# The last sequence's GEGLU in two parts, and the steps of the sequence before it drawn into the last slots

## The chip, the cores and the metric

The kernel runs on one NeuronCore of a Trainium2 chip, in one launch. The metric is the device time of a whole execution, in microseconds (us); where several runs are given, it is their median. The engines are TensorE (PE, with its weight loads PEld), VectorE (DVE), ScalarE (ACT), GpSimd (POOL) and SyncE (SP), each of which takes its instructions in the order in which the program issues them.

## What is computed

The input x is 4 sequences of 512 tokens with 128 features, float32. It is cut here to what matters:

```python
x = x + attention(layernorm(x), Wq, Wk, Wv, Wr)     # 16 heads of 64, causal penalty
y = layernorm(x)
for i in range(6):
    y = local_attention_layer(shift_tokens(y), Wqkv[i], ...) + y   # windows of 32 tokens
    y = ffn_layer(shift_tokens(y), ...) + y
return x + y

def ffn_layer(x, g, bln, W1, b1, W2, b2):
    mu = x.mean(-1, keepdims=True)
    var = ((x - mu) ** 2).mean(-1, keepdims=True)
    xn = (x - mu) / jnp.sqrt(var + 1e-05) * g + bln
    a, gate = jnp.split(xn @ W1 + b1, 2, -1)        # 341 columns each
    return a * jax.nn.gelu(gate, approximate=False) @ W2 + b2
```

`shift_tokens` takes the upper 64 features of a token from the token before it in the same sequence. So the FFN of a tile of tokens needs the tile itself and the last column of the tile before it.

## The kernel before

Stage 1 (to about 590 us) is the first attention layer. It isn't touched. Stage 2 is the six layers. Its work is cut into 96 units, one for each layer, sequence and tile of 128 tokens (6 x 4 x 4), numbered in this order; `u.T` is the tile within its sequence. Activations lie transposed, features on the partitions and tokens along the free axis: `xT[b]` is 128 x 512.

The order of the work is written out by hand. `slot(n, ...)` issues, in a software pipeline, the attention of unit n (scores, softmax, times_v), the projections and rotations of unit n+2, the transposes of q and k of unit n+1, and the output projection (`project_out_2`, L633) and residual (L641) of unit n-1. `scores` (L565, L576) ends with two DVE operations, the row maximum mx (L586) and the subtraction to pr (L588); then ACT takes the exponent (L594), PE transposes pr (L538, the helper `transposed`, whose copies on ACT are L541), and `times_v` (L608, and on DVE L617, L618) forms the output, which `transpose_o` transposes into aT.

The rotations of unit n+2 run on DVE (L463, L467) and POOL (L478 adds the two halves, L486 multiplies with the inverse norm; both on 128 x 1024). POOL also takes the 12 operations (L82 to L85) of the inverse root of the norms and the carry of k (L557). `rsqrt` is three Newton steps: two integer operations on DVE, then four operations three times on the engine given.

The FFN of a sequence (class `Ffn`) is seven steps over all four tiles at once, one step in each slot after the sequence's last unit n (in slots n+1 to n+7): `shift` (POOL, L416 to L418), `mean` (PE L93, DVE L95, ACT Square L97), `var` (PE L102, DVE L104 and the 14 operations of `rsqrt`), `scale` (PE L110, DVE L114, L116) together with GEGLU chunk 0, chunk 1, chunk 2, and `out`. A chunk is two matmuls (L666 for the gate, L667), a Gelu on ACT (L669) and a multiply on DVE (L671); chunks have 128, 128 and 85 rows. Each 128 x 512 float32 matmul is two passes in the trace. `out` is three matmuls (L680) and an addition (L682). In the last layer, `finish` follows it: an addition of x1T (L691), four transposes (L694), a copy on ACT (L696) and a store of 256 KB on SP (L697). Gelu and Exp need different tables of ACT, so a change from one to the other brings an ACT_TABLE_LOAD.

In a slot, `shift`, `mean`, `var` and `scale` stand after the residual, that is behind mx and pr of the slot's unit; the chunks and `out` stand at the slot's end, before `transpose_o`. The slots run to 102. Sequence 22 (layer 5, b = 2) shifts in slot 92 and ends in 98; sequence 23 shifts in slot 96, when all attention is issued, and ends in 102. From slot 94 on there is no unit n+2 left to project. In the profile, slot 94 begins at 2246.7 us (L565) and slot 95 at 2265.25.

PSUM: `one_t` gives one of two banks in turn, `two_t(k, ...)` one of three pairs of banks, counted from n. SBUF: `tmpt` gives one of 7 tiles in turn; the tags rot, t1 and pr have 6, 3 and 2 tiles of 128 x 1024.

Of the kernel before, what the change touches and what calls it, by code (L numbers as in the profile page):

```python
# [8 lines left out]
F32 = mybir.dt.float32  # L9
BF16 = mybir.dt.bfloat16  # L10
I32 = mybir.dt.int32
AF = mybir.ActivationFunctionType
ALU = mybir.AluOpType
# [18 lines left out]
def body(ctx: ExitStack, tc: tile.TileContext, a, out: bass.AP):  # L32
# [16 lines left out]
    def tmpt(n=S):  # L49
        return tmp.tile([P, n], F32, tag="tmp", name="tmp_t")  # L50
# [22 lines left out]

    def rsqrt(v, n, eng):

        y = small.tile([P, n], F32, tag=f"y{n}", name="y")
        t = small.tile([P, n], F32, tag=f"yt{n}", name="yt")
        ti = t.bitcast(I32)
        nc.vector.tensor_scalar(ti, v.bitcast(I32), 1, None, ALU.logical_shift_right)  # L79
        nc.vector.tensor_scalar(y.bitcast(I32), ti, -1.0, 1597463007.0, ALU.mult, ALU.add)  # L80
        for k in range(3):
            eng.tensor_tensor(t, y, y, ALU.mult)  # L82
            eng.tensor_tensor(t, t, v, ALU.mult)
            eng.tensor_scalar(t, t, -0.5, 1.5, ALU.mult, ALU.add)
            eng.tensor_tensor(y if k < 2 else v, y, t, ALU.mult)  # L85

    def layernorm_steps(state, bank, inT, outT, g=None, b=None):

        def mean():
            m = bank()
            mm(m, lhsT=avg, rhs=inT(), start=True, stop=True)  # L93
            xc = state["xc"] = tmpt()
            nc.vector.tensor_tensor(xc, inT(), m, ALU.subtract)  # L95
            sq = state["sq"] = tmpt()
            nc.scalar.activation(sq, xc, AF.Square)  # L97

        def var():
            v = bank()  # L100
            for t in range(NT):
                mm(v[:, t : t + 1], lhsT=state["sq"][:, t * P : (t + 1) * P], rhs=avg[:, 0:1], start=True, stop=True)  # L102
            rs = state["rs"] = small.tile([P, NT], F32, tag="rs", name="rs")
            nc.vector.tensor_scalar(rs, v[:, 0:NT], EPS, None, ALU.add)  # L104
            rsqrt(rs, NT, nc.vector)

        def scale():
            bc = bank()
            for t in range(NT):
                nc.tensor.transpose(  # L110
                    bc[:, t * P : (t + 1) * P], state["rs"][:, t : t + 1].to_broadcast([P, P]), ident
                )
            h = state["h"] = outT()
            nc.vector.tensor_tensor(h, state["xc"], bc, ALU.mult)  # L114
            if g is not None:
                nc.vector.tensor_scalar(h, h, g, b, ALU.mult, ALU.add)  # L116

        return mean, var, scale
# [13 lines left out]
    with tc.tile_pool(name="s1", bufs=1) as s1, tc.tile_pool(  # L132
# [71 lines left out]
        class Rows:  # L204


            def __init__(self, b, c, t):
                self.b, self.c, self.t = b, c, t
# [202 lines left out]
    def flat(pt):  # L411
        return pt.rearrange("p a n -> p (a n)")

    def shift_into(dst, src):

        nc.gpsimd.memset(dst[HD:P, 0:1], 0.0)  # L416
        nc.gpsimd.tensor_copy(dst[0:HD, :], src[0:HD, :])
        nc.gpsimd.tensor_copy(dst[HD:P, 1:S], src[HD:P, 0 : S - 1])  # L418

    def layer_tables(i):  # L420

# [222 lines left out]


    class Ffn:
        def __init__(self, i, b):
            self.i, self.b, self.us, self.st = i, b, [], {}
            self.mean, self.var, self.scale = layernorm_steps(
                self.st,  # L650
                one_t,
                lambda: self.xs,
                lambda: s2.tile([P, S], F32, tag="hT", name="hT", bufs=2),
                vecs[:, i, 0:1],
                vecs[:, i, 1:2],
            )

        def shift(self):
            self.xs = tmpt()
            shift_into(self.xs, xT[self.b])  # L660

        def chunk(self, f):
            i, (f0, fn), h = self.i, FCH[f], self.st["h"]
            w1 = ffn_w[0][0]
            gp = two_t(0, "ps_proj")
            mm(gp[0:fn, 0, :], lhsT=w1[:, DH + f0 : DH + f0 + fn], rhs=h, start=True, stop=True)  # L666
            mm(gp[0:fn, 1, :], lhsT=w1[:, f0 : f0 + fn], rhs=h, start=True, stop=True)  # L667
            g = tmpt()
            nc.scalar.activation(g[0:fn, :], gp[0:fn, 0, :], AF.Gelu, bias=vecs[0:fn, i, 6 + f : 7 + f])  # L669
            u = tmpt()  # L670
            nc.vector.scalar_tensor_tensor(  # L671
                u[0:fn, :], gp[0:fn, 1, :], vecs[0:fn, i, 3 + f : 4 + f], g[0:fn, :], ALU.add, ALU.mult
            )
            self.us.append(u)

        def out(self):
            w2 = ffn_w[0][1]
            y = two_t(0, "ps_proj")[:, 0, :]
            for f, (f0, fn) in enumerate(FCH):
                mm(y, lhsT=w2[0:fn, f, :], rhs=self.us[f][0:fn, :], start=(f == 0), stop=(f == len(FCH) - 1))  # L680
            xn = new_xT()
            nc.vector.scalar_tensor_tensor(xn, y, vecs[:, self.i, 2:3], xT[self.b], ALU.add, ALU.add)  # L682
            xT[self.b] = xn
            if self.i + 1 == L:
                self.finish(xn)
            elif self.b + 1 == B:
                ffn_w[0] = load_ffn(self.i + 1)

        def finish(self, xn):
            fin = tmpt()  # L690
            nc.vector.tensor_tensor(fin, x1T[self.b], xn, ALU.add)  # L691
            op = one_t()
            for t in range(NT):
                nc.tensor.transpose(op[:, t * P : (t + 1) * P], fin[:, t * P : (t + 1) * P], ident)  # L694
            ot = tmpt()
            nc.scalar.copy(ot, op)  # L696
            nc.sync.dma_start(  # L697
                out=out[self.b].rearrange("(t p) e -> p t e", p=P),
                in_=ot.rearrange("p (t e) -> p t e", e=EMB),
            )  # L700

# [25 lines left out]
        if u.b + 1 == B and u.T + 1 == NT and u.i + 1 < L:  # L727
            wpart[j] = load_part(u.i + 1, j)

    def slot(n, now, last):  # L730

        u, prev, nxt, new = unit(n), unit(n - 1), unit(n + 1), unit(n + 2)
        T = n % NT
        part[0] = n % 3
        begin(unit(n + 4))
        if u:
# [11 lines left out]
            sum_squares(new, 0)  # L750
        if prev:
            residual(prev)
        if now and T > 0:
            (now.mean, now.var, now.scale)[T - 1]()
        if now and T == 0:
            now.shift()
        if new:
            rotate(new, 0)
            do_project(new, 2)
# [23 lines left out]
            over_norm(new, 1)  # L783
        if nxt:
            carry_k(nxt, follower(nxt))
        if now and T == 3:
            now.chunk(0)
        if last:
            (lambda: last.chunk(1), lambda: last.chunk(2), last.out)[T]()
        if u:  # L790
            transpose_o(u)

    with tc.manual_schedule():
        begin(units[0])
        ffns = {}
        late = norm_x1(one_t, B - 1)
        for n in range(-2, len(units) + NT + 3):
            if -2 <= n < 1:
                late[n + 2]()
            q = n // NT - 1  # L800
            if n % NT == 0 and 0 <= q < L * B:
                ffns[q] = Ffn(units[n - 1].i, units[n - 1].b)
            slot(n, ffns.get(q), ffns.pop(q - 1, None) if n % NT == 2 else ffns.get(q - 1))

def _constants(n):

# [90 lines left out]
```

## Time and profile before

| | |
|---|---|
| time, median of 3 runs | 2316.82 us (2313.41 to 2319.04) |
| time of the profiled execution | 2314.14 us |
| its span, first to last instruction | 2312.4 us |
| mean granted TensorE clock | 0.993 |
| PE, DVE, ACT, POOL busy | 95%, 74%, 56%, 62% of the span |
| output stores | 4 of 256 KB, on SP |

The end of the span, by stretches (us busy of each engine, and the clock granted to TensorE as a share of full speed):

| stretch | PE | DVE | ACT | POOL | clock |
|---|---|---|---|---|---|
| 2240 to 2250 | 9.26 | 7.48 | 7.08 | 5.03 | 1.00 |
| 2250 to 2260 | 8.83 | 8.22 | 4.28 | 5.09 | 1.00 |
| 2260 to 2270 | 8.09 | 4.03 | 1.87 | 0.09 | 0.83 |
| 2270 to 2280 | 7.58 | 2.99 | 3.30 | 0.00 | 0.66 |
| 2280 to 2290 | 9.62 | 3.43 | 3.65 | 1.22 | 1.00 |
| 2290 to 2300 | 6.51 | 4.67 | 0.87 | 0.00 | 0.85 |
| 2300 to 2313 | 6.86 | 3.69 | 2.36 | 0.00 | 0.89 |

A line of the timeline has the start, the duration (of a merged group: to the end of its last), the engine, the line of the code, the operation, what it writes and reads, shapes and count. A line of the chain has start, duration, engine, what is written, line and count. The busy time of PE isn't work at full rate: at half the clock the same matmul counts twice as long.

### The profile page before, as it was taken

What the parts mean: (1) busy time and instruction counts of PE and PEld (TensorE: products, weight loads), DVE (VectorE), ACT (ScalarE), POOL (GpSimd) and SP (SyncE); (2) the same over time, 40 slices, a digit from 0 to 9 for tenths busy, and PEclk for the clock granted to TensorE, in tenths of its full rate; (3) what the DMA queues carried; (4) which work ended last, traced back from release to release, by engine and by line L of the source; (5) the groups of instructions that cost most, each with busy time, mean ns of one, the idle gap of its engine ahead of it and who ended that gap; (6) DMA issues with size and microseconds to landing.
All of it is one profiled execution on the core that took longest, in us unless ns stands there. A gap on an engine that the chain in (4) does not pass through costs nothing.

```text
span 2312.4 us, 81596 instructions
## 1 busy us (share of the span) xinstructions
PE 2201.3 (95%) x35088; PEld 1447.7 (63%) x35088; DVE 1710.5 (74%) x2692; ACT 1301.7 (56%) x2166; POOL 1436.1 (62%) x1897
## 2 busy tenths in 40 slices
PE   6999999999799999999999999999999999999997
PEld 3555555555366666666666666666666666666664
DVE  3665656656678788878877888877888788878773
ACT  2554544445255666666666666666566666566662
POOL 1443444444577777766767766767776767766760
PEclk9999999999999999999999999999999999999998
DMA  3000000000222233222322223223332223322220
GB/s 113 1 1 1 1 1 1 1 1 1 46 69 68 63 90 75 62 69 65 90 71 65 71 66 90 68 63 73 73 89 62 71 62 86 80 62 72 66 56 15
DMA packets 91025, 125.81 MB, mean 54 GB/s; under 512 B 25262, under 2 KB 39468, under 8 KB 90668
## 3 DMA queue, kind: packets, MB, share of 16 engines
q1 hardware_dynamic: 90236, 119.02, 21.0%
q8 instruction: 279, 4.57, 0.9%
q10 hardware_dynamic: 432, 1.57, 0.2%
q14 instruction: 78, 0.64, 0.1%
HBM read 20.41 MB, written 1.05 MB: 9 GB/s over the span
## 4 chain that ended last, share of the span: by engine, by line
PE 81%; DVE 14%; ACT 2%; issue 2%; POOL 1%; DMA 1%; SPq 0%; POOLq 0%; ACTq 0%
PE ps_proj L442 19%; PE ps_one L538 13%; PE ps_one L633 7%; PE ps_att L608 6%; PE ps_att L576 6%; PE ps_sc L216 5%; PE ps_o L287 5%; PE ps_pt L270 3%; PE ps_proj L666 3%; PE ps_proj L667 3%; PE ps_proj L680 2%; DVE yt L79 2%; PE ps_sc L229 2%; DVE t L467 2%; DVE rot L463 2%
## 5 line engine op out<-in xcount | busy, mean ns | idle before, releaser
L478 POOL TENSOR_TENSOR rot<-rot,t 128x1024 f32<-128x1024 f32 x192 | 453.9, 2364 | 193.9 <-DVE t L467 188.6
L442 PE MATMUL ps_proj<-wqkv,xs 128*128 128x512 f32 x1152 | 557.5, 607 | 15.3 <-DVE t L467 5.4
L259 POOL TENSOR_TENSOR pr<-pr,den 128x1024 f32<-128x1024 f32 x128 | 240.9, 1893 | 335.3 <-DVE den L256 333.1
L453 ACT ACTIVATE sq<-ps_proj 128x1024 f32<-128x1024 f32 x192 | 196.9, 1025 | 365.9 <-PE ps_proj L442 329.3
L486 POOL TENSOR_TENSOR rot<-rot,ss 128x1024 f32<-128x1024 f32 x192 | 365.4, 1903 | 15.0
L442 PEld LDWEIGHTS ps_proj<-wqkv,xs 128*128 128x128 f32 x1152 | 200.0, 192 | 179.6 <-issue 156.6
L458 DVE TENSOR_REDUCE ss<-sq 128x16 f32<-128x1024 f32 x192 | 233.1, 1214 | 51.4 <-ACT sq L453 50.7
L241 DVE TENSOR_REDUCE nm<-ps_sc 128x2 f32<-128x1024 f32 x128 | 156.0, 1218 | 118.7 <-PE ps_sc L229 118.7
L463 DVE TENSOR_TENSOR rot<-ps_proj,lt 128x1024 f32<-128x1024 f32 x192 | 233.4, 1216 | 0.0
L467 DVE TENSOR_TENSOR t<-ps_proj,lt 128x1024 f32<-128x1024 f32 x192 | 232.8, 1213 | 0.0
L274 ACT COPY pT<-ps_pt 128x512 f32<-128x512 f32 x128 | 75.2, 588 | 264.6 <-PE ps_pt L270 262.9
L633 PEld LDWEIGHTS ps_one<-aT,wo 128*128 128x128 f32 x1536 | 186.3, 192 | 45.3 <-issue 44.5
L538 PE MATMUL ps_one<-ident,rot 128*128 128x128 f32 x1536 | 210.2, 280 | 2.9 <-issue 1.5
L586 DVE TENSOR_REDUCE mx<-ps_att 128x16 f32<-128x1024 f32 x96 | 117.5, 1224 | 97.1 <-PE ps_att L576 95.3
L633 PE MATMUL ps_one<-aT,wo 128*128 128x128 f32 x1536 | 187.3, 275 | 0.4 <-ACT aT L541 0.4
L247 ACT ACTIVATE pr<-ps_sc,nm 128x512 f32<-128x512 f32 x256 | 175.0, 694 | 16.3 <-DVE nm L241 16.3
L82 POOL TENSOR_TENSOR yt<-y 128x32 f32<-128x32 f32 x288 | 68.9, 239 | 181.8 <-DVE y L80 166.6
L538 PEld LDWEIGHTS ps_one<-ident,rot 128*128 128x128 f32 x1536 | 164.4, 141 | 22.1 <-issue 4.6
L608 PEld LDWEIGHTS ps_att<-vw,pT 64*32 64x32 f32 x9216 | 104.0, 106 | 95.5 <-ACT pT L541 54.0
L270 PEld LDWEIGHTS ps_pt<-ident,pr 128*128 128x128 f32 x1024 | 120.0, 142 | 55.9 <-issue 45.8
L608 PE MATMUL ps_att<-vw,pT 64*32 64x65 f32 x9216 | 129.6, 226 | 26.4 <-DVE t L467 15.9
L520 ACT COPY vt<-ps_proj 128x512 f32<-128x512 f32 x192 | 103.1, 589 | 83.2 <-PE ps_proj L442 82.1
(127 smaller groups left out, 4014.8 us busy)
## 6 DMA issues: line engine op xcount, KB each, us to landing
vw<-vt SPq DMA_DIRECT2D x1152, 65.0 KB
vw_first<-vt SPq DMA_DIRECT2D x336, 65.0 KB
wqkv<-in_wqkv_dram SPq DMA_DIRECT2D x18, 512.0 KB
wo<-in_wo_dram SPq DMA_DIRECT2D x6, 512.0 KB
w<-in_w_dram SPq DMA_DIRECT2D x6, 341.0 KB
xr<-in_x_dram SPq DMA_DIRECT2D x4, 256.0 KB
out_dram<-tmp_t SPq DMA_DIRECT2D x4, 256.0 KB
w<-in_w_dram SPq DMA_DIRECT2D x12, 64.0 KB
```

What stands on the lines that cost most here:

```text
L259: nc.gpsimd.tensor_tensor(self.pr, self.pr, self.den.unsqueeze(2).to_broadcast([P, 2, S]), ALU.mult)
L270: nc.tensor.transpose(pt[:, k * P : (k + 1) * P], self.pr[:, h, k * P : (k + 1) * P], ident)
L442: mm(p[:, c, :], lhsT=u.xs[:, u.T * P : (u.T + 1) * P], rhs=wpart[j][:, c * 512 : (c + 1) * 512], start=True, stop=True,)
L453: nc.scalar.activation(u.sq, u.p[j], AF.Square)
L458: nc.vector.tensor_reduce(u.ss[:, j * HEADS : (j + 1) * HEADS], heads(u.sq), AX.X, ALU.add)
L463: nc.vector.tensor_tensor(heads(t0), heads(pf), lt[:, u.T, 2 * j].unsqueeze(1).to_broadcast([P, HEADS, HD]), ALU.mult)
L467: nc.vector.tensor_tensor(t1.rearrange("p (h t d) -> p h t d", t=2, d=half), pf.rearrange("p (h t d) -> p h t d", t=2, d=half)[:, :, ::-1, :],
L478: nc.gpsimd.tensor_tensor(u.r[j], u.r[j], u.t1, ALU.add)
L486: nc.gpsimd.tensor_tensor(heads(u.r[j]), heads(u.r[j]), u.ss[:, j * HEADS : (j + 1) * HEADS].unsqueeze(2).to_broadcast([P, HEADS, HD]), AL ...
L538: nc.tensor.transpose(tp[:, c * P : (c + 1) * P], src[:, (4 * g + c) * P : (4 * g + c + 1) * P], ident)
L608: mm(o[j * W : (j + 1) * W, h, c * (HD + 1) : (c + 1) * (HD + 1)], lhsT=u.pT[h * HD : (h + 1) * HD, 4 * g + c, j * W : (j + 1) * W], rhs=u ...
L633: mm(y[:, 0:P], lhsT=wo_w[0][:, c, :], rhs=u.aT[:, c, :], start=(c == 0), stop=(c == NC - 1))
```

## The change

`Ffn` takes a range of tiles (`t0`, `nt`), the tiles that it writes to, and the engine of its inverse root; chunks and `out` take the number of their pair of PSUM banks. The steps stand in two tables, `norm` (after the residual) and `geglu` (at the slot's end), filled by `plan`. Up to sequence 21 they stand where they stood.

Sequence 22: `shift` in slot 92 and `mean` in 93 as before; `var` at the end of slot 93 (before: after the residual of 94); `scale` in slot 94, chunks 0 and 1 at the end of 94, chunk 2 at the end of 95, `out` in slot 96.

Sequence 23 is two objects. `most` is its first three tiles: `shift` after the residual of slot 95, `mean` at the end of 95, the rest in slot 96, its inverse root on POOL. `last` is the last tile, all in slot 96, its inverse root on DVE. Their steps are interleaved as the four lines with `plan(norm, end, ...)` say (`end` is 96). Slot 96 is the last. They write to tiles of the tags rot, t1 and pr. `finish` adds in place. The stores become two of 256 KB, one of 192 KB and one of 64 KB. By the listing of each engine's instructions, ACT has two table loads more (Gelu in slot 94, and Exp after it).

```diff
     def rsqrt(v, n, eng):
-        y = small.tile([P, n], F32, tag=f"y{n}", name="y")
-        t = small.tile([P, n], F32, tag=f"yt{n}", name="yt")
+        m = max(n, NT)
+        y = small.tile([P, m], F32, tag=f"y{m}", name="y")[:, 0:n]
+        t = small.tile([P, m], F32, tag=f"yt{m}", name="yt")[:, 0:n]
...
-            rs = state["rs"] = small.tile([P, NT], F32, tag="rs", name="rs")
-            nc.vector.tensor_scalar(rs, v[:, 0:NT], EPS, None, ALU.add)
-            rsqrt(rs, NT, nc.vector)
+            rs = state["rs"] = small.tile([P, NT], F32, tag="rs", name="rs")[:, 0:nt]
+            nc.vector.tensor_scalar(rs, v[:, 0:nt], EPS, None, ALU.add)
+            rsqrt(rs, nt, eng)
...
         def shift(self):
-            self.xs = tmpt()
-            shift_into(self.xs, xT[self.b])
+            n, c0 = self.nt * P, self.t0 * P
+            xs, src = self.temp()[:, 0:n], self.u.xn
+            if c0 == 0:
+                shift_into(xs, src[:, 0:n], n)
+            else:
+                nc.gpsimd.tensor_copy(xs[0:HD, :], src[0:HD, c0 : c0 + n])
+                nc.gpsimd.tensor_copy(xs[HD:P, :], src[HD:P, c0 - 1 : c0 + n - 1])
+            self.xs = xs
...
         def finish(self, xn):
-            fin = tmpt()
-            nc.vector.tensor_tensor(fin, x1T[self.b], xn, ALU.add)
+            n, nt, t0 = self.nt * P, self.nt, self.t0
+            nc.vector.tensor_tensor(xn, x1T[self.b][:, t0 * P : t0 * P + n], xn, ALU.add)
...
-        if now and T > 0:
-            (now.mean, now.var, now.scale)[T - 1]()
-        if now and T == 0:
-            now.shift()
+        for f in norm:
+            f()
...
-        if now and T == 3:
-            now.chunk(0)
-        if last:
-            (lambda: last.chunk(1), lambda: last.chunk(2), last.out)[T]()
+        for f in geglu:
+            f()
         if u:
             transpose_o(u)
...
+        f = Ffn(units[end - NT - 1])
+        plan(norm, end - 4, f.shift)
+        plan(norm, end - 3, f.mean)
+        plan(geglu, end - 3, f.var)
+        plan(norm, end - 2, f.scale)
+        plan(geglu, end - 2, at(f.chunk, 0, 2), at(f.chunk, 1, 0))
+        plan(geglu, end - 1, at(f.chunk, 2, 2))
...
+        def halves(k):
+            t = s2.tile([P, INNER], F32, tag="t1", name="t1", bufs=3)
+            return t[:, 0:S], t[:, S : 2 * S]
...
+        most = Ffn(units[end - 2], 0, NT - 1, big, halves, nc.gpsimd)
+        last = Ffn(units[end - 1], NT - 1, 1, big, sixths)
+        plan(norm, end - 1, most.shift)
+        plan(geglu, end - 1, most.mean)
+        plan(norm, end, last.shift, most.var, at(f.out, 2), most.scale, last.mean, at(most.chunk, 0, 0))
+        plan(norm, end, last.var, at(most.chunk, 1, 1), at(most.chunk, 2, 2), last.scale)
+        plan(norm, end, at(most.out, 0), at(last.chunk, 0, 1), at(last.chunk, 1, 2), at(last.chunk, 2, 0))
+        plan(norm, end, at(last.out, 1))
+        for n in range(-2, end + 1):
             if -2 <= n < 1:
                 late[n + 2]()
-            q = n // NT - 1
-            if n % NT == 0 and 0 <= q < L * B:
-                ffns[q] = Ffn(units[n - 1].i, units[n - 1].b)
-            slot(n, ffns.get(q), ffns.pop(q - 1, None) if n % NT == 2 else ffns.get(q - 1))
+            slot(n, norm.get(n, ()), geglu.get(n, ()))
```

Here `big` gives a tile of the tag rot and `sixths` pairs of 128 columns of one tile of the tag pr; `at(f, *args)` is a call put off.

## The prediction

> **What bounds the kernel now.** I read the page first (PE 95% busy), then the chain of work that ended last, then the timeline of the last 65 us. Up to about 2246 us the two kernels issue the same instructions in the same order, by the listing of each engine's instructions, so only the end can differ. There the chain runs, from 2248.85:
>
> ```profile
> 2248.85 1.24 DVE mx L586
> 2250.11 1.24 DVE pr L588
> 2251.37 1.07 ACT pr L594
> 2252.48 0.67 PE ps_one L538 x4
> ...
> 2258.30 2.63 PE ps_proj L680 x6
> ...
> 2267.37 1.24 DVE mx L586
> ...
> 2278.76 1.48 PE ps_proj L667 x2
> ...
> 2308.56 0.59 ACT tmp_t L696
> ```
>
> Columns: start, duration, engine, what it writes. Without new projections to fill it, PE waits for the softmax of units 94 and 95: from mx to the transposes of pr 3.63 us (2248.85 to 2252.48). The start of mx in slots 94 and 95 therefore sets the end.
>
> The timeline of the same place shows what DVE's small operations meet beside long POOL ones:
>
> ```profile
> 2246.89 0.75 DVE L671 SCALAR_TENSOR_TENSOR tmp_t<-ps_proj,vecs,tmp_t 85x512 f32<-85x512 f32 x1
> 2248.63 1.90 POOL L486 TENSOR_TENSOR rot<-rot,ss 128x1024 f32<-128x1024 f32 x1
> 2250.49 2.35 POOL L478 TENSOR_TENSOR rot<-rot,t 128x1024 f32<-128x1024 f32 x1
> 2251.78 1.08 DVE L79 TENSOR_SCALAR yt<-rs 128x4 int32<-128x4 int32 x1
> 2252.90 0.17 DVE L80 TENSOR_SCALAR y<-yt 128x4 int32<-128x4 int32 x1
> 2252.92 1.91 POOL L486 TENSOR_TENSOR rot<-rot,ss 128x1024 f32<-128x1024 f32 x1
> 2253.11 1.74 DVE L82 TENSOR_TENSOR yt<-y 128x4 f32<-128x4 f32 x1
> 2254.78 0.39 POOL L557 COPY kT<-kT 128x256 f32<-128x256 f32 x1
> 2254.88 0.30 DVE L83 TENSOR_TENSOR yt<-yt,rs 128x4 f32<-128x4 f32 x1
> ```
>
> L79 and L82, 0.17 us elsewhere, last until the POOL operation beside them ends (2252.84, 2254.83). This is the variance step of sequence 22. Its 15 DVE operations take 5.6 us here (2251.58 to 2257.17), and 2.93 us for sequence 23, when POOL is idle (2289.56 to 2292.49). In this place the hold costs nothing: mx has already gone.
>
> Last, single microseconds of PE (PE busy, granted clock, then DMA):
>
> ```profile
> 2262.00:2263.00 1.00, 0.42 (x3) 0.90 0.00 0
> 2263.00:2264.00 1.00, 1.00 (x7) 0.50 0.00 0
> 2277.00:2278.00 1.00, 1.00 (x2) 0.50 0.09 16
> ```
>
> The clock is halved over 2262.9-2266.1, 2273-2279.9 and 2297-2300.3: after each longer idle stretch of PE.
>
> **What the Trainium skill says.** "SBUF — State Buffer", Who interferes with whom: a DVE operation with two SBUF inputs, or in a two-port mode, and a GpSimd operation exclude each other for the whole instruction. The trace agrees: L79 has a median of 1.585 us over 32 instances, against 0.17. "TensorE: Matmul & The Clock Gate", Part 1: the clock is gated to half after an idle window and restored after a busy one, on a free-running grid of 3.41 us. The trace agrees: the changes lie 3.2, 6.9, 6.9, 17.1 and 3.3 us apart, near multiples of 3.41. Where the grid will lie after the change is not known; I keep that of before and give both ends. "ScalarE: Activation LUTs", What ACT_TABLE_LOAD costs: each change of table set is an instruction of ACT; the trace has 1.28 us.
>
> **The change, part by part.** I cut the chain at six points and add what each stretch gains or loses.
>
> 1. *Variance of sequence 22 to the end of slot 93* (start of mx in slot 94). The 15 DVE operations now stand before mx in DVE's queue, behind the L671 that ends at 2247.64. The first four (add of epsilon, two integer operations, one multiply) slip between POOL's small operations, which occupy it until 2248.6. Then POOL runs L486, L478, L486 and L557 without a pause, to 2255.2 and, with the few tenths that it loses itself, about 2255.4. By the fence above, one operation gets through at the end of L486, two at the end of L478 (0.08 us of POOL gap), one after the second L486, one after L557. That leaves 15 - 4 - 5 = 6, at 0.2 us each: 2256.6. Behind the waiting operation stand mx and pr, and for pr wait exp, the transposes and times_v; nothing else is ready for PE but the projection of unit 93. mx starts at 2256.7 instead of 2248.85: **+7.8**. Bounds: +1.9 if POOL holds nothing (2247.64 + 3.0 = 2250.7; the scores end before that, by 2250.4 with the 0.95 us that PE's variance matmuls, L102, put ahead of them), +8.3 if one operation fewer slips through. The removal of the same 15 from slot 94 gains nothing: they ran beside PE's work.
>
> 2. *mx to the end of the third L680 of sequence 21*: 12.08 us before (2248.85 to 2260.93). PE is now idle from about 2252 to 2260.3 but for 0.6 us, so its clock is half when the transposes start. At half clock eight of them take 2.06 (2263.27), against 1.04. Two such groups before a window has passed: **+1.8** (0.5 to 2.5).
>
> 3. *To mx of slot 95*: 6.44 before. Now: residual and final add on DVE with their gaps 1.64 (2260.93 to 2262.57), L694's transposes 0.65, then chunks 0 and 1, eight passes at 0.43 = 3.44, transposes of on 1.04, scores 2.05; sum 8.8. With one half-clock window on the chunks, as before's window after the same wait, 1.7 more: 10.5, **+4.1** (+2.4 with none). Two table loads more (Gelu, then Exp again) lie beside PE's chunks and scores: ACT has 2.0 us for the second; were it late, up to 1.28.
>
> 4. *mx of slot 95 to the end of its GEGLU chunk*: 12.87 before (2267.37 to 2280.24). Chunk 2 replaces chunk 0, four passes either way; the scale step, gone to slot 94, was covered by the softmax: **0** (-3.4 if the half clock of 2273-2279.9 doesn't recur).
>
> 5. *To the end of the output projection of unit 95*: 3.29 before (2280.24 to 2283.53). The aT copies now queue on ACT behind the Square of the three-tile mean. Chunk end, Gelu 0.68, multiply 0.75, subtract 0.55, Square 0.52, copy 0.59, gaps 0.1, projection 2.05: 5.2, **+2.0** (+0.5 if the Square came first). The shift on POOL (three copies, about 1.2) lies beside the softmax.
>
> 6. *To the end of the last ACT copy*: 25.62 before (2283.53 to 2309.15). Now, with widths scaled from 512 columns by the trace's slopes (DVE 0.69 to 0.28 from 512 to 128 columns; a pass 0.43 to 0.32 for 384; Gelu 0.69 to 0.58): variance matmuls 0.7, three DVE operations 0.6; the 12 POOL operations of the inverse root. Those are not in the trace at three columns; with 32 columns they come each 0.32 us, 3.9 in all, and the column slope takes off 0.6 at most; I take 3.6, and 0.7 for the final add L691, which holds POOL for its length as L83 was held at 2191.98 (0.78). rs is ready 5.9 after the projection. Transposes, hT on DVE: 7.5. Chunk 0, 1.3, at half clock 2.6: 10.1. Gelu and multiply 1.2; then the last tile's inverse root, 15 DVE operations, 2.95, before the multiplies of chunks 1 and 2: 14.25. PE's transpose of it and the three W2 products, 2.2: 16.45. DVE 1.2, transposes 0.6, then the last tile: 12 passes 1.55, Gelu and multiply 0.7, W2 0.3, two adds 0.65, transpose and copy 0.6, gaps 0.2: **22.0**, so **-3.6** (-4.9 with a full clock, -2.5 with the dearer POOL).
>
> 7. *The last store*: issued at 2309.17, the span ends at 2312.4. It carries 64 KB instead of 256; the other 192 KB leave 3 us earlier. **-0.4** (0 to -0.7). SP has nothing else queued: its last v-window transfer is issued at 2248. The pools lend tiles whose readers have finished; no wait there.
>
> Sum: 7.8 + 1.8 + 4.1 + 0 + 2.0 - 3.6 - 0.4 = **+11.7**. On the profiled execution that is a span of 2312.4 + 11.7 = 2324.1 and a time of 2314.14 + 11.7 = 2325.8; that execution lies 2.7 below the median of the runs, so I predict 2316.82 + 11.7 = **2328.5**.
>
> **Rivals.** *POOL doesn't hold the chain, the clock as above*: step 1 is +1.9 and step 2 is 0, in sum +4.0: 2320.8. For it: the DVE operations need the shared port for a tenth of a microsecond each. Against it: L79 and L82 above. Chance 0.10. *Not slower: PE keeps its full clock.* If POOL doesn't hold DVE, mx starts at 2250.7 and PE never idles long before the end: steps 1.9 + 0 + 2.4 - 3.4 + 2.0 - 4.9 - 0.4 = -2.4: 2314.4. It decides if mx of slot 94 starts before about 2251. Against it: PE's idle 1.6 us ahead of L694 remains. Chance 0.07. *Half clock everywhere*: with the grid badly placed two more windows fall on PE-bound work, on times_v of unit 94 and on chunks 1 and 2 of the three tiles, at 1.7 us each, and the Exp table comes 1.3 late: +16.4: 2333.2. For it: before has a double window in slot 95. Against: each of these stretches is busy. Chance 0.08. That the change does nothing is excluded: the listing shows the moves.
>
> **How the numbers follow.** The forecast has the remaining 0.75, with its own range 2322 to 2333: step 3 without its window (-1.7), step 4 with half of its gain (-1.7) and step 6 at full clock (-1.3), not all at once, below; step 6's dearer end (+1.1), step 2's (+0.7) and a late table load (+1.3) above, widened by the 2.8 by which the runs of before lie around their median. From 2319 to 2334 leaves out the second rival and the edge of others: under 0.2. A difference of 0.2% (4.6 us) is about what a measurement of this kernel can tell from none. Slower by more: the forecast nearly whole, the third rival and some of the first, 0.82; within: 0.15; faster: the best edge of the second, 0.03.
>
> **What would show it.** Right: in slot 93 to 94 variance operations of 1.5 us and more among the 15, mx about 9 us after the multiply of the chunk before it; PE idle 8 us ahead of the transposes of pr at half clock; aT copies of unit 95 after a Square; about 22 us from the last projection to the last copy. Wrong: 15 operations in 3 us and mx right behind the scores; or the last stretch under 18 us.

## The result and the profile after

The changed kernel takes 2322.38 us (median of 16 runs, 2316.55 to 2326.57) against 2317.58 for the kernel before beside it (16 runs): ratio 1.0022, 95% interval 1.0012 to 1.0032. It is slower, as forecast, and the time lies in the range, but the loss is 4.8 us and not 11.7.

The busy shares are those of before (PE 95%, DVE 74%, ACT 56%, POOL 62%), on a span of 2318.2 us (profiled execution 2320.18). The traces, one execution of each kernel, say more once both are cut at the points of the prediction. S0 is the start of DVE's multiply of sequence 21's last chunk in slot 93 (L671 before, L684 after); all that either kernel issues ahead of it is the same.

| stretch (step of the prediction) | before | after | difference | predicted |
|---|---|---|---|---|
| start to S0 | 2246.89 | 2249.67 | +2.78 | 0 |
| 1: S0 to mx of slot 94 | 1.96 | 9.02 | +7.06 | +7.8 |
| 2: to the end of sequence 21's `out` | 12.07 | 12.67 | +0.60 | +1.8 |
| 3: to mx of slot 95 | 6.45 | 8.25 | +1.80 | +4.1 |
| 4: to the end of slot 95's chunk | 12.86 | 9.05 | -3.81 | 0 |
| 5: to the end of the last output projection | 3.30 | 5.10 | +1.80 | +2.0 |
| 6: to the end of the last ACT copy | 25.62 | 22.04 | -3.58 | -3.6 |
| 7: to the end | 3.25 | 2.40 | -0.85 | -0.4 |
| sum of 1 to 7 | 65.51 | 68.53 | +3.02 | +11.7 |

Over the twelve kernels of this study S0 lies between 2246.18 and 2252.17, without order between those that begin with the same instructions: the first row is scatter of the runs, and the seven steps are what the change does.

The timeline of after in slots 93 and 94, its lines of DVE and POOL alone, shows step 1. Columns: start, duration, engine, line, operation:

```profile
2249.67 0.75 DVE L684 SCALAR_TENSOR_TENSOR tmp_t<-ps_proj,vecs,tmp_t 85x512 f32<-85x512 f32 x1
...
2251.42 1.91 POOL L489 TENSOR_TENSOR rot<-rot,ss 128x1024 f32<-128x1024 f32 x1
2251.60 1.75 DVE L86 TENSOR_TENSOR y<-y,yt 128x4 f32<-128x4 f32 x1
2253.29 2.35 POOL L481 TENSOR_TENSOR rot<-rot,t 128x1024 f32<-128x1024 f32 x1
2253.38 2.28 DVE L83 TENSOR_TENSOR yt<-y 128x4 f32<-128x4 f32 x1
...
2255.72 1.91 POOL L489 TENSOR_TENSOR rot<-rot,ss 128x1024 f32<-128x1024 f32 x1
2255.89 1.76 DVE L85 TENSOR_SCALAR yt<-yt 128x4 f32<-128x4 f32 x1
...
2258.69 1.22 DVE L589 TENSOR_REDUCE mx<-ps_att 128x16 f32<-128x1024 f32 x1
```

Three operations on four columns take 1.75, 2.28 and 1.76 us, each to the end of the POOL operation beside it, and between two POOL operations one or two get through. mx, next in DVE's queue, starts 9.02 us after the multiply instead of 1.96. The chain that ended last is now this queue, then what waits for it:

```profile
2258.77 1.15 DVE mx L589
...
2262.31 1.97 PE ps_one L541 x8
...
2268.78 2.59 PE ps_proj L693 x6
...
2279.61 1.24 DVE mx L589
...
2287.80 0.87 PE ps_proj L680 x2
...
2315.53 0.27 ACT rot L711
```

Two times in it answer the two lines of the kernel before that the prediction showed at 2278.76 and 2258.30: `out` of sequence 21 takes 2.59 instead of 2.63, and the last two passes of slot 95's chunk (L680 here) 0.87 instead of the 1.48 of L667 there. So PE runs at full speed in slot 95, where the kernel before ran at half. Single microseconds of PE in after (busy, granted clock, DMA) say so too:

```profile
2260.00:2261.00 1.00, 0.01 (x1) 0.50 0.00 0
...
2272.00:2273.00 1.00, 0.00 (x0) 1.00 0.00 0
...
2286.00:2287.00 1.00, 1.00 (x79) 1.00 0.00 0
```

The clock falls while PE waits for the late mx (half from 2258.8 to 2265.7), and then not until 2299.8: neither after the 1.66 us of idle ahead of L709 nor after the softmax of slot 95.

### The profile page after: what moved, and what is told of

It is laid out like the page before. It is cut to its first block, busy times and chain, and to the rows that moved or that the text cites. A ratio compares the mean times of both kernels' runs of the same rounds, so it can differ in the third digit from the quotient of the medians.

```text
span 2318.2 us, 81636 instructions
## 1 busy us (share of the span) xinstructions
PE 2195.8 (95%) x35076; PEld 1448.5 (62%) x35108; DVE 1716.9 (74%) x2703; ACT 1305.6 (56%) x2173; POOL 1441.1 (62%) x1911
## 4 chain that ended last, share of the span: by engine, by line
PE 80%; DVE 14%; issue 2%; ACT 2%; POOL 1%; SPq 1%; DMA 1%; POOLq 0%; ACTq 0%
PE ps_proj L445 19%; PE ps_one L541 13%; PE ps_one L636 7%; PE ps_att L611 6%; PE ps_att L579 6%; PE ps_sc L219 5%; PE ps_o L290 5%; PE ps_pt L273 3%; PE ps_proj L693 2%; PE ps_proj L679 2%; PE ps_proj L680 2%; DVE yt L80 2%; DVE t L470 2%; DVE rot L466 2%; PE ps_sc L232 1%
## 5 line engine op out<-in xcount | busy, mean ns | idle before, releaser
L83 POOL TENSOR_TENSOR yt<-y 128x32 f32<-128x32 f32 (+1 forms) x291 | 69.9, 240 | 181.6 <-DVE y L81 166.2
```

## The experiments

The theory: the variance of sequence 22 in slot 93 costs 7 us, held by POOL; the split end gives back about 4; between them the clock decides some us either way. Rivals: the delay only takes the place of a wait that would come anyway; the end is short for another reason than the split; the clock is a consequence and costs nothing by itself. "Before" in what follows is the kernel before, timed on the same chip beside each.

### e1: the variance back in slot 94

```diff
-        plan(geglu, end - 3, f.var)
-        plan(norm, end - 2, f.scale)
+        plan(norm, end - 2, f.var)
+        geglu[end - 2].insert(0, f.scale)
```

> The changed kernel with one part undone: the variance of sequence 22 goes back behind mx, pr and the residual of slot 94, and its scale step moves to the end of slot 94, ahead of the output of sequence 21. Theory (the 15 DVE operations are held by POOL in front of mx): mx of slot 94 starts about 2 us after the multiply of the chunk before it, as in the kernel before, instead of 9; PE then has no long idle stretch; the time falls by about 7 us against the changed kernel, to about 2315.5, 0.999 of the kernel before. Rival (the loss is in the two chunks and two table loads drawn into slot 94, the hold lies beside other waits): within 1.5 us of the changed kernel, about 2322.

Measured: 2315.24 us against 2318.61, ratio 0.9986 (0.998 to 0.9993). Step 1 is back at 1.93. In the timeline mx now follows the scores, with nothing on DVE between:

```profile
2250.45 0.75 DVE L684 SCALAR_TENSOR_TENSOR tmp_t<-ps_proj,vecs,tmp_t 85x512 f32<-85x512 f32 x1
...
2252.38 1.23 DVE L589 TENSOR_REDUCE mx<-ps_att 128x16 f32<-128x1024 f32 x1 [1.18 <-PE ps_att L579]
```

Of the 7.09 us that step 1 wins against the changed kernel, step 2 takes back 1.44 (14.11); the others stay within 0.1. That isn't the price of the variance inside step 2, which was there in the kernel before too (12.07). It is the clock: it is half from 2257.57 to 2260.98, while PE has work all the time, and the first 64 matmuls of times_v take 1.97 us there, the other 64 0.86 at full clock.

```profile
2257.34 1.97 PE L611 MATMUL ps_att<-vw,pT 64*32 64x65 f32 x64 [0.24 <-ACT pT L544]
...
2257.57:2260.98 3.41, 3.41 (x72) 0.50 0.02 5
```

The second line is PE in that stretch (busy, granted clock, DMA). With fillers and full clock (e10, below) the same order takes 12.92 in step 2. Without this one move (the scale step goes with it) the change is faster than the kernel before.

### e2: the kernel before with that one move

```diff
-        if now and T > 0:
+        if now and T > 0 and n != 94:
             (now.mean, now.var, now.scale)[T - 1]()
...
             (lambda: last.chunk(1), lambda: last.chunk(2), last.out)[T]()
+        if n == 93:
+            now.var()
```

> The kernel before with one part of the change alone: the variance of sequence 22 stands at the end of slot 93, behind the chunk, instead of behind the residual of slot 94. Nothing else moves. Theory (hold by POOL in front of mx): mx of slot 94 starts 7 us later, and the whole end with it, since nothing of it is used earlier: 2317.6 + 7 to 7.7 = about 2325, 1.0032 of the kernel before. Rival (the moved variance is hidden, the change loses elsewhere): within 1.5 us of the kernel before.

Measured: 2325.26 us against 2318.61, ratio 1.0033 (1.0021 to 1.0046): +6.65. Step 1 is 9.01, as in the changed kernel. So the loss belongs to the move and not to its company. Steps 2, 5 and 6 are each 1.3 to 1.7 longer than before; the traced execution, 2329.97 us, is the slowest of the five, so not all of that is typical. The clock is half over 2258.5-2268.7, 2275.5-2278.9, 2285.8-2292.6 and 2309.7-2316.5. In step 5 it is a table load of 1.28 that in the other traces lies beside times_v, and here starts only with the Gelu that needs it (2293.09). Step 4 stays at 13.09, with a pause of PE that the prediction had not told apart from the half clock. PE's timeline in e2 (in brackets the idle time ahead and what ended it):

```profile
2288.92 0.66 PE L608 MATMUL ps_att<-vw,pT 64*32 64x65 f32 x23 [1.45 <-issue]
```

The kernel before has the same pause, and the changed kernel does the 128 matmuls in one go (first line before, second after):

```profile
2276.10 0.66 PE L608 MATMUL ps_att<-vw,pT 64*32 64x65 f32 x23 [1.17 <-issue]
2284.57 2.22 PE L611 MATMUL ps_att<-vw,pT 64*32 64x65 f32 x128 [0.24 <-ACT pT L544]
```

In before and e2 it stands in times_v of unit 95 with 23 of its 128 matmuls to go, and no semaphore that the profile shows ends it. No trace of the changed order has this pause in slot 95. What ends it is told in the part on the prediction.

### e3: same place, the inverse root kept in PSUM

If POOL holds DVE by the SBUF operands and not by the place in the queue, operations with one operand in PSUM should pass. The Newton steps are written so that none reads two tensors from SBUF; where y is needed in both memories it is computed twice, so there are 18 operations, counting the addition of epsilon, instead of 15.

```diff
+    def rsqrt_psum(rs, ps):
+        v, i, p, q = (ps[:, c : c + NT] for c in (16, 32, 48, 64))
...
+        for k in range(3):
+            nc.vector.tensor_tensor(t, p, s, ALU.mult)
+            nc.vector.tensor_tensor(q, v, t, ALU.mult)
+            nc.vector.tensor_scalar(t, q, -0.5, 1.5, ALU.mult, ALU.add)
+            for y in (s, p) if k < 2 else (rs,):
+                nc.vector.tensor_tensor(y, p, t, ALU.mult)
...
-        f = Ffn(units[end - NT - 1])
+        f = Ffn(units[end - NT - 1], vbank=lambda: two_t(2, "ps_proj")[:, 0, :])
```

> The changed kernel, variance of sequence 22 in the same place, but its inverse root keeps its numbers in PSUM so that no DVE operation of it has more than one SBUF input or SBUF alone on both sides; 18 operations instead of 15. Theory (POOL holds DVE over the SBUF port that they share): no operation of the chain lasts over 0.4 us although POOL runs the same long operations, the chain takes about 3.7 us, mx starts about 5 us earlier than in the changed kernel, the time is about 2317. Rival (the small operations are slow for another reason, their order or their waits on each other): single operations of 1.5 us and more stay, the time is about 2322.5.

Measured: 2315.40 us against 2318.61, ratio 0.9989 (0.998 to 0.9998). Its timeline at the same place (lines of the code lie some 15 further on):

```profile
2253.93 1.90 POOL L504 TENSOR_TENSOR rot<-rot,ss 128x1024 f32<-128x1024 f32 x1
2254.06 0.16 DVE L97 TENSOR_TENSOR yt<-ps_proj,y 128x4 f32<-128x4 f32 x1
...
2255.78 2.35 POOL L496 TENSOR_TENSOR rot<-rot,t 128x1024 f32<-128x1024 f32 x1
2255.80 0.16 DVE L97 TENSOR_TENSOR yt<-ps_proj,y 128x4 f32<-128x4 f32 x1
...
2256.94 1.23 DVE L604 TENSOR_REDUCE mx<-ps_att 128x16 f32<-128x1024 f32 x1 [0.38 <-PE ps_att L594]
```

With POOL busy beside them from 2253.93 on, no operation takes more than 0.17 us. mx comes 4.77 us after the multiply, and what ends last ahead of it is PE's scores: the matmuls of the variance (L120) had waited there for DVE's t (L485, a rotation), and the scores stand behind them. The hold is thus shown from both sides: away with the place (e1), away with the operands (e3).

### e4: sequence 23 in one piece

```diff
-        most = Ffn(units[end - 2], 0, NT - 1, big, halves, nc.gpsimd)
-        last = Ffn(units[end - 1], NT - 1, 1, big, sixths)
...
+        most = Ffn(units[end - 1], 0, NT, big, halves, nc.gpsimd)
+        plan(norm, end, most.shift, at(f.out, 2), most.mean, most.var, most.scale)
+        plan(norm, end, at(most.chunk, 0, 0), at(most.chunk, 1, 1), at(most.chunk, 2, 2), at(most.out, 0))
```

> The changed kernel with the other part undone: sequence 23 in one piece of four tiles, all in slot 96, its inverse root on POOL; sequence 22 as in the changed kernel. My reckoning: without the mean ahead of the aT copies the projection of unit 95 ends about 1.5 us earlier; from there to the last ACT copy about 23.3 us instead of 22.0; the last store is of 256 KB again, 0.8 us longer: in sum within 1.5 us of the changed kernel, 2322 to 2324. Rival (the split is what wins the end stretch, 3.6 us against the kernel before): 2325 to 2327.

Measured: 2329.79 us against 2318.61, ratio 1.0047 (1.0034 to 1.006). This was a miss: I expected the split to be worth about nothing, and the time lies above both forecasts. Step 5 falls back to 3.30 (no Square ahead of the copies), but step 6 is 28.20 against 22.04. Its chain shows why it is longer than even the kernel before's 25.62:

```profile
2296.00 2.05 PE ps_one L636 x16
...
2302.93 0.87 PE ps_one L96 x2
...
2312.87 2.07 PE ps_proj L679 x2
```

In this order the mean (L96) stands behind `out` of sequence 22 and its transposes, which wait for two DVE additions: it starts 4.9 us after the projection. The clock is half from 2307.3 to 2317.6, so the chunks start there at 2.07 for two passes. The split, which computes the three-tile mean ahead of the last projection, is 6.2 us shorter in step 6 than this order and pays 1.8 in step 5. Part of the 6.2 is the clock: PE is busy for 5.8 us at half clock in e4's step 6 (2307.32 to 2317.56) and for 3.25 in after's (2299.79 to 2303.20), which makes about 1.3 us by an estimate that counts half of such time as lost.

### e5 and e6: filler matmuls in PE's idle stretches

If the clock costs something by itself, matmuls whose result is overwritten, put into idle stretches of PE, should give time. e5 is the kernel before with six 128x512 ones: two ahead of the transposes of `finish` for b = 1 and 2, one ahead of the transposes of pr in slots 94 and 95. e6 is the changed kernel with the same, a second one in slot 94, and four ahead of the transposes (L113) of sequence 22's `scale`.

```diff
+    def warm(bank, k):
+        for _ in range(k):
+            mm(bank, lhsT=avg, rhs=tabs.rearrange("p t f d -> p (t f d)")[:, 0:512], start=True, stop=True)
...
         tp = one_t()
+        warm(tp, fill)
...
             op = one_t()
+            warm(op, 2 if self.b in (1, 2) else 0)
```

> The kernel before with six matmuls of 128x512 added on PE in its idle stretches of the end, into PSUM banks that the transposes behind them overwrite: two ahead of L694 of sequences 21 and 22, one ahead of the transposes of pr in slots 94 and 95. Only the clock can gain by it. Theory (the kernel before loses to half-clock windows that the changed kernel mostly doesn't have; that is why my steps 3 and 4 came out too dear): no half clock up to the last hT; the stretch from out of sequence 21 to mx of slot 95 falls from 6.4 to about 5.1 us, from there to the end of the chunk from 12.9 to 9 to 10.3, the end by another 1 to 1.7: about 5 us in all, 2313, 0.998. Rival (the clock is beside other waits, the difference of these stretches is in the order of the work): within 1.5 us of the kernel before.

> The changed kernel with eleven such matmuls in its idle stretches: four ahead of the transposes of the inverse root of sequence 22, two and one ahead of the transposes of pr of units 94 and 95, two ahead of L709 of sequences 21 and 22. Theory: half clock goes in slot 94, where PE mostly waits anyhow (0.6 us), and in chunk 0 of the three tiles (1.3): 2 us in all, 2320.5. If the clock weighed as much here as my prediction had it (5 us and more): 2317.

Measured: e5 2311.88 us against 2316.59, ratio 0.998 (0.9973 to 0.9987): more work in 4.7 us less. Step 3 is 5.26 instead of 6.45, step 4 is 10.94 instead of 12.86. Single microseconds of PE in e5:

```profile
2275.00:2276.00 1.00, 1.00 (x87) 1.00 0.00 0
...
2297.00:2298.00 1.00, 1.00 (x2) 0.50 0.00 0
```

The windows over the transposes of `finish` and over slot 95 are gone; the one near 2297, where no filler stands, remained, and step 6 is 25.63 as before. The pause of PE isn't gone; it has moved into the output projection of unit 94, still within step 4:

```profile
2270.14 1.49 PE L639 MATMUL ps_one<-aT,wo 128*128 128x128 f32 x11 [1.37 <-issue]
```

e6: 2319.76 us, ratio 1.0012 (1.0006 to 1.0019). No half clock before 2311; step 6 is 20.83, but step 2 is 12.83 against 12.67: ahead of the transposes of pr the fillers, it seems, take the time that they save. With fillers in both, the changed kernel is 7.9 us slower than the kernel before (e6 against e5): step 1, still 9.02, stays, the gain of step 4 shrinks from 3.8 to 1.9, and the loss of step 3 grows from 1.8 to 2.9.

### e7: the Square behind the aT copies

```diff
+            if not late:
+                square()
+        def square():
             sq = state["sq"] = temp()[:, 0:w]
-            nc.scalar.activation(sq, xc, AF.Square)
+            nc.scalar.activation(sq, state["xc"], AF.Square)
         def var():
+            if late:
+                square()
...
-        most = Ffn(units[end - 2], 0, NT - 1, big, halves, nc.gpsimd)
+        most = Ffn(units[end - 2], 0, NT - 1, big, halves, nc.gpsimd, True)
```

> The changed kernel with the Square of the three-tile mean behind the aT copies of unit 95 on ACT instead of ahead of them. Theory (step 5: the aT copies wait for it): from the end of chunk 2 to the end of the projection 3.3 to 3.8 us instead of 5.1; the Square lies beside the projection; 1.5 us in all, 2321. Rival (something else is late there, so nothing is won): 2322.4.

Measured: 2320.54 us against 2316.59, ratio 1.002 (1.0013 to 1.0026). Step 5 is 4.31 instead of 5.10; half of what the Square was held responsible for. In the changed kernel the copies stood behind it:

```profile
2290.66 0.53 ACT L100 ACTIVATE rot<-rot 128x384 f32<-128x384 f32 x1 [1.27 <-DVE rot L98]
2291.09 1.05 ACT L544 COPY aT<-ps_one 128x512 f32<-128x512 f32 x2
```

With the Square gone, the next in line shows (e7, lines some 6 further on):

```profile
2287.97 0.59 ACT L550 COPY aT<-ps_one 128x512 f32<-128x512 f32 x1 [0.45 <-PE ps_one L547]
2288.61 0.66 PE L547 MATMUL ps_one<-ident,on 128*128 128x128 f32 x4 [0.73 <-ACT aT L550]
```

The second half of the transposes waits for the first copy to clear its PSUM bank: two rounds of transpose and copy, where the copies had stood back to back.

### e8: the last tile's inverse root on POOL

```diff
-        last = Ffn(units[end - 1], NT - 1, 1, big, sixths)
+        last = Ffn(units[end - 1], NT - 1, 1, big, sixths, nc.gpsimd)
...
-        plan(norm, end, last.var, at(most.chunk, 1, 1), at(most.chunk, 2, 2), last.scale)
-        plan(norm, end, at(most.out, 0), at(last.chunk, 0, 1), at(last.chunk, 1, 2), at(last.chunk, 2, 0))
+        plan(norm, end, last.var, at(most.chunk, 1, 1), at(most.chunk, 2, 2), at(most.out, 0), last.scale)
+        plan(norm, end, at(last.chunk, 0, 1), at(last.chunk, 1, 2), at(last.chunk, 2, 0))
```

> The changed kernel with the inverse root of the last tile on POOL and its scale step behind the output of the three tiles, so that the 15 DVE operations don't stand ahead of the multiplies of chunks 1 and 2. Theory (step 6: they hold the W2 products): the products end about 1.6 us earlier, of which the last tile's later hT takes back 0.5 to 0.8: the stretch from the last projection to the last copy 21 us instead of 22, 2321.5. Rival (PE's chunks are the bound there): within 0.3 us in the trace.

Measured: 2323.83 us against 2316.59, ratio 1.0035 (1.0021 to 1.0048); a miss. The three-tile part does win: its W2 products end 15.25 us after the projection instead of 16.1. But the last tile's hT (the scaled input of its chunks) is now made behind it. The end of e8's chain:

```profile
2316.26 0.55 PE ps_one L709 x3
...
2318.54 0.43 PE ps_proj L680 x2
...
2323.25 0.27 ACT rot L711
```

From L709 to the end of the last copy it is 7.26 us (2316.26 to 2323.52) instead of 4.66 (2311.14 to 2315.80 in after): hT (L117 and L119, 2316.95 to 2317.64) stands on the path, and PE, idle meanwhile, does the chunks at half clock (2317 to 2321), 0.43 for two passes instead of 0.22. Step 6 is 23.81.

### e9 and e10: the best of each

e9 is the changed kernel with the edits of e3, e7 and six fillers as in e5; e10 has e1's instead of e3's.

> What the runs point to, put together: the changed kernel with the inverse root of sequence 22 in PSUM, the Square behind the aT copies, and six matmuls of 128x512 in idle stretches of PE (one ahead of the transposes of pr in slots 94 and 95, two ahead of L709 of sequences 21 and 22). From the measured stretches: multiply of the chunk to mx 4.8, then 12.1, 8.2, 9.1, 4.3, 20.9, 2.4 = 61.8 us, 3.7 less than the kernel before in its trace and 6.7 less than the changed kernel: about 2312. Should the gains cover the same waits, about 2315, as with the inverse root in PSUM alone.

> The same with the variance of sequence 22 back in slot 94 instead of in PSUM: from the measured stretches 1.9, 12.7 (14.1 less its half-clock window), 8.2, 9.1, 4.3, 20.9, 2.4 = 59.5 us, 6 less than the kernel before: about 2311. Should the gains cover the same waits, about 2315.

Measured: e9 2313.43 us, ratio 0.9991 (0.9983 to 1.0), not clear of the noise; e10 2310.49 us against 2315.0, ratio 0.9979 (0.9971 to 0.9986). e10 is faster than both kernels. But it isn't shown to be faster than the old order with six fillers: e5 has the ratio 0.998 (0.9973 to 0.9987), so the fillers may be the whole of the gain, and what the rebuilt end adds to them is not shown. From S0 the end of e10 takes 60.26 us in its trace, against 65.51 in the kernel before, 68.53 after and 62.46 in e5. All stretches of all traces (us):

| | 1 | 2 | 3 | 4 | 5 | 6 | 7 | sum |
|---|---|---|---|---|---|---|---|---|
| before | 1.96 | 12.07 | 6.45 | 12.86 | 3.30 | 25.62 | 3.25 | 65.51 |
| after | 9.02 | 12.67 | 8.25 | 9.05 | 5.10 | 22.04 | 2.40 | 68.53 |
| e1 | 1.93 | 14.11 | 8.26 | 9.05 | 5.10 | 22.14 | 2.46 | 63.05 |
| e2 | 9.01 | 13.35 | 6.37 | 13.09 | 4.64 | 27.32 | 3.23 | 77.01 |
| e3 | 4.77 | 12.04 | 9.94 | 10.33 | 5.10 | 21.91 | 2.44 | 66.53 |
| e4 | 9.00 | 13.62 | 9.95 | 10.45 | 3.30 | 28.20 | 3.25 | 77.77 |
| e5 | 1.81 | 12.25 | 5.26 | 10.94 | 3.30 | 25.63 | 3.27 | 62.46 |
| e6 | 9.02 | 12.83 | 8.19 | 9.05 | 5.10 | 20.83 | 2.40 | 67.42 |
| e7 | 9.02 | 12.78 | 8.25 | 9.13 | 4.31 | 22.20 | 2.40 | 68.09 |
| e8 | 9.00 | 13.38 | 9.94 | 10.34 | 5.09 | 23.81 | 2.38 | 73.94 |
| e9 | 4.30 | 11.98 | 8.19 | 9.05 | 4.31 | 20.82 | 2.36 | 61.01 |
| e10 | 2.48 | 12.92 | 8.19 | 9.13 | 4.31 | 20.82 | 2.41 | 60.26 |

## Where the prediction was right and where wrong

The direction and its mechanism were right: the variance in slot 93 is held by POOL and delays mx, and the end gives back less than that. The size was not: 11.7 forecast, 4.8 measured by the medians, 3.0 by the seven steps of the traces. Of the 8.7 between 11.7 and 3.0, steps 2, 3 and 4 hold 7.3. The steps that failed are step 4, whose half clock was taken to recur, and the half-clock window of step 3.

*Step 1*, +7.06 for +7.8. Right, shown by e1, e2 and e3; six operations, not four, got through ahead of POOL's long ones. "SBUF — State Buffer", Who interferes with whom, of the Trainium skill names two SBUF inputs, or a two-port mode, as what excludes the other engine; after and e3 agree, with 1.75 to 2.28 us beside POOL for operations wholly in SBUF (L85 has one input only), and 0.17 us and less for every operation with an operand in PSUM. Without the hold, as e3 has it, step 1 is still +2.81, through PE's matmuls of the variance ahead of the scores; the prediction had +1.9 for no hold.

*Step 2*, +0.60 for +1.8. The half clock at the transposes came as said, but it lasted to 2265.7 only, two windows, and 0.60 is at the low end of the bounds. In e4 and e8, whose instructions are the same up to there, it lasted three, and the step took 13.62 and 13.38.

*Step 3*, +1.80 for +4.1. Its term "one half-clock window on the chunks ... 1.7 more" didn't come: the stretch took 8.25, which is 0.55 less than the sum without the window (8.8), mostly because the scores took 1.68 us (2277.89 to 2279.57) and not 2.05. e3, e4 and e8 did get the window, at 9.94, 9.95 and 9.94, 1.7 more, with the clock at half over 2270.95-2274.36 in e3. So its price was right and its coming was not certain: of the six kernels with the changed order and no fillers, three have it (e3, e4, e8) and three don't (after, e1, e7).

*Step 4*, -3.81 for 0: the largest error. The prediction gave -3.4 "if the half clock of 2273-2279.9 doesn't recur", and chose that it would. It didn't, and neither did the pause of PE, which the 3.4 had counted as half clock. From the traces: times_v's 128 matmuls take 2.59 and 0.66 before, with the pause between, and 2.22 after, 1.03 less; the four passes of the chunk take 3.55 before (2276.68 to 2280.23) and 1.95 after (2286.71 to 2288.66), so 1.60 less; the pause is 1.17. Together 3.80 of the 3.81. In e3, e4 and e8 the step is 10.3 to 10.5: one half window, no pause. So the changed order is 2.4 to 3.8 us shorter here in all six of its traces without fillers; but that is a gain of clock and pause, and fillers bring half of it to the kernel before too (e5, 10.94).

What failed in both is not the grid of the clock's windows that the prediction kept. "TensorE: Matmul & The Clock Gate", Part 1, of the Trainium skill has windows on a free-running grid; in these two traces it lies alike. The changes of the clock at 2262.79 before and 2258.83 after come 15.90 and 9.16 us behind S0; the difference is 6.74, two windows of 3.41 within 0.1. What failed is that the windows of before were carried over to the same places in the work, without asking how the delayed waits would fall on the grid. PE's wait ahead of the transposes of `finish` (L694, L709) is 1.66 us in before, after and e3 alike. These are the window with most of the wait and the next, in before, e3 and after (PE busy, clock, DMA):

```profile
2259.38:2262.79 3.41, 1.75 (x6) 1.00 0.00 0
2262.79:2266.20 3.41, 3.41 (x60) 0.50 0.26 77
...
2267.54:2270.95 3.41, 1.75 (x7) 1.00 0.00 0
2270.95:2274.36 3.41, 3.41 (x7) 0.50 0.25 77
...
2269.07:2272.48 3.41, 2.29 (x6) 1.00 0.00 0
2272.48:2275.89 3.41, 2.87 (x10) 1.00 0.19 56
```

In before, e2, e3, e4 and e8 the first edge of the grid comes 1.87 to 2.24 us after the end of sequence 21's `out`. The wait then lies in one window, PE is busy for 51% of it, and the next is at half clock. In after, e1 and e7 the edge comes after 1.12 to 1.31 us and cuts the wait; the window is 62 to 67% busy, and the clock stays full. Where the page speaks of an idle window, a half-busy one was enough here. On the kept grid the prediction's own times put the wait whole into one window; as steps 1 and 2 came 1.9 us shorter, an edge fell into it. The share alone isn't a rule: in e1 half clock followed a window that was 67% busy (2254.16 to 2257.57).

So one trace of a kernel gives steps 2 to 4 only to some 4 us. Four kernels issue the same instructions on PE up to slot 95's chunk: after, e4, e7 and e8. In steps 1 to 4 they take 5.65, 9.68, 5.84 and 9.32 us more than the one trace of before, 7.6 in the mean. With steps 5 to 7 as measured (-2.63) that gives +5.0, an estimate made afterwards, beside the 4.8 of the medians. By that the trace of after, with its 3.0, is likely one of the lucky ones. It fits that its granted clock, 0.994, is the highest of the kernel's sixteen executions (0.987 to 0.994), though that is a mean over the whole execution and doesn't say where.

*Step 5*, +1.80 for +2.0: right in size, but the working named one wait where there are two. e7 takes the Square away and keeps 1.0 of the 1.8.

*Step 6*, -3.58 for -3.6, with the half window at 2299.8-2303.2 that was reckoned with; e6 without it is 1.2 shorter, for 1.3 forecast. The split carries it (e4). That the number is met to 0.02 is luck in part: the terms named for the inverse root add up to 5.6 and not 5.9 (5.1 in the trace), and those of the last part to 22.25 and not 22.0. *Step 7*, -0.85 for -0.4, beyond its bound of -0.7: the stretch behind the last copy ends 2.4 us after it with 64 KB, 3.25 with 256 KB.

The rivals: "POOL doesn't hold the chain" gave 2320.8, near the measured 2322.4, for a wrong reason, as its step 1 of +1.9 against 7.06 shows; a single time could not have told them apart. "PE keeps its full clock" was half right: the clock was kept in slot 95, though mx came late. "Half clock everywhere" didn't come: from slot 94 to the last copy after has it over 2258.8-2265.7 and 2299.8-2303.2 only. The two table loads that the change adds in slot 94 lie beside PE's work in after (2274.29 and 2278.79, the second done before pr is), as reckoned.

*The pause of PE* is 1.17 to 1.45 us in three traces, lies in times_v of unit 95 in two and in the output projection of unit 94 in the third, and no semaphore ends it. The DMA records show what comes just before: a transfer of 16 KB on the queue of the kind "instruction". Its line in before, from the DMA view of 2273 to 2276:

```profile
q8 instruction: 1, 0.02, 2.2%
```

It lands at 2274.79, and PE goes on 1.31 us later; in e2 and e5 it lands at 2287.54 and 2268.73, and PE goes on 1.38 and 1.41 later. These transfers come every 6.6 us on average. All 262 pauses of PE in the twelve traces after 610 us that are 0.35 us or longer and that no semaphore ends, end 1.19 to 1.65 us after such a landing. So PE very likely waited for its own instructions; no run changes that by itself. In after the transfer lands at 2281.71, while PE waits for the softmax anyway. And in before the pause prolonged the half clock, if the pattern of these traces holds: the window with it (2273.03 to 2276.44) is 65% busy, and the next is at half clock too, as it is in the twelve traces after each later half-clock window (from 630 us on) that is 75% busy or less, and after none that is 81% or more.

## What to carry to other kernels

Before a chain of small DVE operations is moved ahead of something that PE waits for, look at what POOL runs in the new place: beside back-to-back long POOL operations each small one whose operands are all in SBUF can last as long as POOL's. If it must stand there, keep one operand in PSUM. A half-clock window seen in one trace must not be carried over to the same place of the work: reckon where the delayed waits fall between the edges of the windows, for each place of the edges, and forecast the window at its chance. And try a few filler matmuls in PE's waits before anything is rebuilt: here six of them in the old order gave the same ratio as the best rebuilt end.

## What the runs showed of the hardware

- A DVE operation on 128x4 with all operands in SBUF took up to 2.28 us beside POOL; 18 operations with an operand in PSUM took 0.16 to 0.17 us each in the same place.
- The same wait of PE, 1.66 us, brought a half-clock window of 3.41 us where it lay in one window of the grid (51% busy, five traces) and none where an edge cut it (62 to 67%, three traces).
- Pauses of PE that no semaphore ended were over 1.19 to 1.65 us after the landing of a 16 KB instruction transfer, 262 of 262; in step 4 of before, e2 and e5 they took 1.17, 1.45 and 1.37 us.
- Six matmuls that compute nothing made the kernel before faster, 0.998 (0.9973 to 0.9987). Where they stand ahead of work that is ready soon they win nothing: step 2 of e6 is 12.83 against 12.67.
- On POOL, the inverse root's operations on 128x4 take 0.19 to 0.20 us each at 0.28 from one to the next (e4, 2307.03 to 2310.33), against 0.15 to 0.16 at 0.19 on DVE alone, on 128x1 (after, 2304.86 to 2307.52).
- The load of an ACT table isn't always made as early as it could be: the same load stood beside times_v in the kernel before (2272.78, 7.5 us ahead of its Gelu) and right ahead of its Gelu in e2, where it cost step 5 1.3 us:

```profile
2293.09 1.28 ACT L669 ACT_TABLE_LOAD   x1 [7.77 <-PE ps_proj L667]
```
